# A decoder layer on one core: the feed-forward products of two heads by seven block products

## The chip, the cores and the metric

The kernel runs on one core of a Trainium2 chip. The core has five engines, each with its own instruction queue: TensorE (PE, matrix products; the loading of its stationary operand is shown apart as PEld), VectorE (DVE), ScalarE (ACT), GpSimd (POOL) and SyncE (SP, which here only issues transfers). They wait for one another by semaphores. TensorE writes to PSUM[...]; the other data lies in SBUF.

The metric is the device time of one execution, in microseconds. The kernel before took 1421.27 us (median of 3 runs, 1421.15 to 1422.03).

## The reference

The layer has 16 sequences of 256 tokens with 512 features. Cut to what matters:

```python
x = layernorm(x + attn(x))           # projections, short convolution, scan
y = causal_conv(v[i] * ctx[j], k) + skip * v[i] * ctx[j]
out[j] = sum_i y[i, j] * ctx[i]      # 8 x 8 pairs in each of 32 heads
x = layernorm(x + out)
base   = x @ W.T + b
logits = x @ gate_w.T + gate_b       # 8 experts
gates  = softmax(top_2(logits))
x = layernorm(base + sum_e gates[e] * (x @ A[e].T) @ B[e].T)
```

All of it is float32. The last three lines are the feed-forward part. For one head its main product is 128 tokens by 512 features by 512 outputs.

## The kernel before

The first part (up to about 750 us) works on groups of 512 tokens: projections, convolution, scan, output product. It already multiplies large matrices by seven block products in place of eight (lines 328 to 374), and the change does not touch it.

The second part is the loop at line 1232 over h = 0 to 31. A head here is 8 feature rows times 16 sequences, that is 128 tokens. Each iteration works on two heads at once: on the cross products of head h, and on the feed-forward part of head f = h - 1. An iteration has two halves, for two halves q of the batch. The instructions of an engine run in the order in which the loop writes them; the kernel sets that order itself, and no scheduler moves them.

One iteration, engine by engine:

* TensorE turns v of head h + 1 (`turned_v`, L147), multiplies the last two row blocks of the feed-forward product of the head before (`feed_forward`, L1227), turns its gates (`turned_gates`, L1217), begins the convolution with a shared product, the seed (L1012), adds the low-rank part (`lora`, L1223), and convolves: four full 128 x 128 products (L1030) and twelve quadrants of 64 x 64 (L1045). Then the second half: logits and low-rank inputs of head f into the tile gl (L1193), first row block (L1227), seed, second row block, and again four full products and twelve quadrants.
* VectorE multiplies the finished convolution by the context and sums it (`multiplied` L1080, `reduced` L1090, for both halves), finishes the feed-forward result of an earlier head (`finish`, L1151), makes the products of the next head (L157, twice), and computes the gates (L1118 to L1138).
* ScalarE copies turned tiles to SBUF (L149, L1219), copies the seed to another bank in two halves (`spread_seed`, L1019), squares for the norms (L1181, L1108) and scales the result that is stored (`store`, L1161).
* GpSimd adds the residual (L1260), folds the squares (L1185), multiplies and adds the skip term (L949 to L967), prepares the next head's sums (xs L996, Td L1001, sk L932), and does the small steps of the norms (L1103 to L1111, L1156, L1212).

Two rules of order matter below. A seed goes to bank 3 of y, `spread_seed` copies it from there to bank 2, and the second full product of the convolution adds to bank 3, so it has to wait until the copies have read it. And y has one buffer of two tiles, y0 and y1 (four banks): a convolution can start only when VectorE's multiplications have read the one before.

[...] four banks for y, two for the pool `ps_t` (gl and the turned gates), one for the turned v (`vp`) and one for the feed-forward result (`base`), both in `ps_b`.

In the gates the eight logits lg of each token are compared with one another (two comparisons, L1127 and L1128, of 128 x 64 elements); both operands are the same tile in SBUF.

Of the kernel before, what the change touches and what calls it, by code (L numbers as in the profile page):

```python
# [14 lines left out]
P = 128  # L15
# [57 lines left out]
def decoder_kernel(  # L73
# [842 lines left out]
    with ExitStack() as s2:  # L916
# [90 lines left out]
        def seeded(y, T, xs, q, apart=False):  # L1007

            seed = bank_of(y, 3)
            if apart:  # L1010
                seed = ps_b.tile([P, BQ * NH * NH], F32, tag="base", name="yc")
            nc.tensor.matmul(seed, T[:, SHARED_AT, :], xs[:, q], start=True, stop=True)  # L1012
            return seed
# [6 lines left out]

        def convolve(y, kv, T, Td, q, between=None, late=False, early=None, ahead=None):

# [45 lines left out]
            if late:  # L1068
                for n, (lb, mb) in enumerate(FIRST if ahead is None else AHEAD):
                    if n == 0 and ahead is not None:  # L1070
                        ahead()
                    if n == 1 and early is not None:
                        early()
                    if n == 3 and between is not None:
                        between()
                    full(lb, mb, T[:, FULL_AT[lb, mb], :])
# [23 lines left out]
        def centred_squares(src, total, tag, between=None):  # L1100

            nm = p2.tile([P, 1], F32, tag=f"nm_{tag}", name=f"nm_{tag}")
            nc.gpsimd.tensor_scalar(nm, total, -1.0 / D, None, ALU.mult)  # L1103
            if between is not None:
                between()
            sq = p2.tile([P, D], F32, tag="sq", name="sq")
            var = p2.tile([P, 1], F32, tag=f"var_{tag}", name=f"var_{tag}")
            nc.scalar.activation(sq, src, AF.Square, bias=nm, accum_out=var)  # L1108
            rs = p2.tile([P, 1], F32, tag=f"rs_{tag}", name=f"rs_{tag}")
            nc.gpsimd.tensor_scalar(var, var, 1.0 / D, LN_EPS, ALU.mult, ALU.add)  # L1110
            nc.gpsimd.tensor_tensor(rs, var, nhalf[:, 0:1], ALU.pow)  # L1111
            return nm, rs

        def gates(gl, rs, room):


            lg = p2.tile([P, NE], F32, tag="lg", name="lg")
            nc.vector.scalar_tensor_tensor(lg, gl[:, 0:NE], rs, gb_bc, ALU.mult, ALU.add)  # L1118
            nm = p2.tile([P, 1], F32, tag="nm", name="nm")
# [4 lines left out]
            own = lg.unsqueeze(2).to_broadcast(sq)  # L1124
            other = lg.unsqueeze(1).to_broadcast(sq)
            cmp = room.rearrange("p (a two b) -> p a two b", two=2, b=NE)
            nc.vector.tensor_tensor(cmp[:, :, 1, :], other, own, ALU.is_equal)  # L1127
            nc.vector.tensor_tensor(cmp[:, :, 0, :], other, own, ALU.is_gt)  # L1128
            nc.vector.tensor_tensor(cmp[:, :, 1, :], cmp[:, :, 1, :], tri, ALU.mult)
            rank = p2.tile([P, NE], F32, tag="rank", name="rank")  # L1130
            nc.vector.tensor_reduce(rank, cmp, AX.XY, ALU.add)
# [15 lines left out]

        def finish(h, base, rs, between=None):
            x3 = p2.tile([P, D], F32, tag="x3", name="x3")
            total = p2.tile([P, 1], F32, tag="sum_c", name="sum_c")  # L1150
            nc.vector.scalar_tensor_tensor(  # L1151
                x3, base, rs, b_bc, ALU.mult, ALU.add, accum_out=total
            )
            nm, rs = centred_squares(x3, total, "c", between)
            nb = p2.tile([P, 1], F32, tag="nb", name="nb")
            nc.gpsimd.tensor_tensor(nb, nm, rs, ALU.mult)  # L1156
            return h, x3, nb, rs
# [15 lines left out]
        def ahead():  # L1173
            vT_ahead.append(turned_v(vns.pop(0), ps_b, "vp"))
            vns.append(load_v(2))
            cTs.append(load_c(2))
# [12 lines left out]
        def products_with_gates(o_l, sq):  # L1189

            gl = ps_t.tile([P, NG + 2 + 2 * NE * NE], F32, tag="tr", name="gl")
            for kc in range(KD):
# [12 lines left out]
        def spread_of(gl, m2):  # L1205
# [4 lines left out]
            )  # L1210
            rs = p2.tile([P, 1], F32, tag="rs_b", name="rs_b")
            nc.gpsimd.tensor_tensor(rs, var, nhalf[:, 0:1], ALU.pow)  # L1212
            return rs

        def turned_gates(xa, at=None):
            xat = (at or ps_t).tile([ER, P], F32, tag="vp" if at else "tr", name="xat")
            nc.tensor.transpose(xat, xa.rearrange("p e r -> p (e r)"), ident)  # L1217
            xaT = p2.tile([ER, P], F32, tag="xaT", name="xaT")
            nc.scalar.copy(xaT, xat)  # L1219
            return xaT  # L1220

        def lora(base, turned):
            nc.tensor.matmul(base, turned[0], w_lb, start=False, stop=True)  # L1223

        def feed_forward(base, o_l, kcs, first=False):
            for kc in kcs:
                nc.tensor.matmul(  # L1227
                    base, o_l[:, kc, :], w_f[:, kc, :], start=(first and kc == kcs[0]), stop=False
                )

        last, done, rest = None, None, None
        for h in range(HX):
            nxt, ff = h + 1 < HX, last is not None
            (kv, T), cT, vT = kvs.pop(0), cTs.pop(0), vT_next
# [6 lines left out]
            if h:  # L1241
                if nxt:
                    v_after = turned_v(vns.pop(0), ps_b, "vp")
                    kvs.append(load_T(h + 1))
                    if h + 2 < HX:
                        vns.append(load_v(h + 2))
                        cTs.append(load_c(h + 2))
                if rest is not None:
                    base, o_r, xa = rest
                    feed_forward(base, o_r, (2, 3))  # L1250
                    turned = turned_gates(xa)
                seed = seeded(y, T, xs, 0, h == 1)
                spread_seed(y, seed, h == 1)
                if rest is not None:
                    lora(base, [turned])
            if ff:
                for i, pr in zip(order, prs):
                    reduced(pr, red_f, 1, i)
                o_l = p2.tile([P, NL, P], F32, tag="ol", name="ol")
                nc.gpsimd.tensor_tensor(  # L1260
# [5 lines left out]
                sq, folded = squares(o_l)  # L1266
            if done is not None:
                ready = finish(*done, folded)
            else:
                ready = None  # L1270
                if ff:
                    folded()
            red = p2.tile([P, NQ, NL, BQ * NH], F32, tag="red", name="red")
            convolve(y, kv, T, Td, 0, late=h == 0, ahead=None if h else ahead)
# [4 lines left out]
            if nxt:  # L1279
                kv_n, T_n = kvs[0]  # L1280
                cT_n, (vT_next, v_n, kept) = cTs[0], v_after
                if h:
                    behind = products(v_n, cT_n, kv_n, 0, kept=kept)
            skips = []

# [10 lines left out]
            y = new_y()  # L1296

            def meanwhile():
                skips.append(skip_term(cT, ws, behind))

            meanwhile()
            o = with_residual(skips[0], vT)
            if ff:
                gl, m2 = products_with_gates(o_l, sq)
                rs = spread_of(gl, m2)
                base = ps_b.tile([P, D], F32, tag="base", name="base")
                feed_forward(base, o_l, (0,), True)
            if nxt:
                seed = seeded(y, T, xs, 1, h == 0)
            if ff:  # L1310
                feed_forward(base, o_l, (1,) if nxt else (1, 2, 3))
            if ready is not None:
                store(*ready)
            if nxt:
                spread_seed(y, seed, h == 0)
# [7 lines left out]
            if ff:  # L1323
                xa = gates(gl, rs, gl[:, NG + 2 :])
            if nxt:
                convolve(y, kv, T, Td, 1)
                rest = (base, o_l, xa) if ff else None
            else:
                turned = []
                y.append(ps_t.tile([P, BQ * NH * NH], F32, tag="tr", name="y2"))  # L1330
                convolve(
                    y, kv, T, Td, 1, lambda: lora(base, turned), True,
                    lambda: turned.append(turned_gates(xa, ps_b)),
                )
            if ff:
                done = (h - 1, base, rs)
            last = (o, red, y, cT)
# [3 lines left out]
        tr = ps_t.tile([P, KD, P], F32, tag="tr", name="tr")  # L1341
        gl = ps_b.tile([P, NG + 2 * NE * NE], F32, tag="vp", name="gl")
        o_l = {}
# [48 lines left out]
        contracted(y_f[0], (0, 1))  # L1392
        ready = finish(*done)
        base = ps_b.tile([P, D], F32, tag="base", name="base")
        contracted(y_f[2].unsqueeze(1), (2,))
        contracted(y_f[1][:, 1:2, :], (3,))
        norms_and_gates(0, 1)
# [4 lines left out]
        _, rs = layer_norm_stats(nc, p2, nhalf, tr.rearrange("p c l -> p (c l)"), "b")  # L1402
        xaT = turned_gates(gates(gl, rs, gl[:, NG:]))
        store(*ready)
        nc.tensor.matmul(base, xaT, w_lb, start=False, stop=True, skip_group_check=True)
# [81 lines left out]
```

## Time and profile before

| | |
|---|---|
| Median of the runs | 1421.27 us |
| The profiled execution | 1421.88 us |
| Its span, first to last instruction | 1420.1 us |
| Granted TensorE clock | 0.998 |
| TensorE busy | 1405.9 us (99%), 6882 records |
| VectorE busy | 1191.5 us (84%) |
| GpSimd busy | 492.1 us (35%); 350.2 of the 600 us from 800 to 1400 |
| ScalarE busy | 415.0 us (29%) |
| One iteration of the loop (1014.37 to 1034.77) | 20.40 us |

How to read it: a float32 product shows as two records on TensorE. Its records overlap, since their ends are modelled, so the time that a product takes is read from one start to the next, not from its duration. "Idle before" is the time in which an engine had nothing to run, with the instruction that ended the wait. In timelines the columns are start, duration, engine, line, operation, output and inputs, shapes, count of merged instructions.

### The profile page before, as it was taken

How to read it: one execution, taken by the hardware profiler on the slowest of the kernel's cores; microseconds unless marked ns; L12 is line 12 of the kernel's file. 1: busy time of each engine (PE TensorE's matmuls, PEld its weight loads, DVE VectorE, ACT ScalarE, POOL GpSimd, SP SyncE). 2: the span in 40 equal slices, each digit the busy share in tenths (PEclk: the TensorE clock that was granted, in tenths of full speed). 3: DMA queues.
4: the chain of work that ended last, by engine and by line, in shares of the span. 5: the costliest groups of instructions: out<-in, count | busy, mean ns of one | idle time of the engine just before them, and what ended most of it. 6: DMA issues, size and time to landing. Idle time of an engine off the chain costs nothing.

```text
span 1420.1 us, 18821 instructions
## 1 busy us (share of the span) xinstructions
PE 1405.9 (99%) x6882; PEld 906.5 (64%) x6882; DVE 1191.5 (84%) x2133; ACT 415.0 (29%) x902; POOL 492.1 (35%) x662
## 2 busy tenths in 40 slices
PE   8999999999999999999999999999999999999997
PEld 7888888787888888888884444444444444444443
DVE  6988878888888787877858988898889889888986
ACT  2423323233232332332311323222322232222321
POOL 5450011110100201001004565556555655565562
PEclk9999999999999999999999999999999999999999
DMA  8013111120211201212003212221222122112200
GB/s 302 33 38 132 35 57 45 38 84 8 60 67 40 73 19 39 84 35 94 16 16 108 67 45 75 68 72 48 75 67 67 53 75 67 63 57 68 74 27 23
DMA packets 49164, 89.15 MB, mean 63 GB/s; under 512 B 8880, under 2 KB 13360, under 8 KB 49072
## 3 DMA queue, kind: packets, MB, share of 16 engines
q1 hardware_dynamic: 49072, 87.96, 19.6%
q8 instruction: 54, 0.88, 0.3%
q14 instruction: 38, 0.31, 0.1%
HBM read 70.62 MB, written 17.32 MB: 62 GB/s over the span
## 4 chain that ended last, share of the span: by engine, by line
PE 97%; DVE 1%; issue 1%; DMA 1%; SPq 0%; POOL 0%; POOLq 0%; ACT 0%; DVEq 0%
PE mm L330 21%; PE y L1030 15%; PE s L330 14%; PE y L1045 12%; PE base L1227 8%; PE s L782 6%; PE mm L782 6%; PE y L1012 4%; PE gl L1193 2%; PE base L1223 2%; PE tr L147 1%; PE xm L599 1%; PE mm L739 1%; PE mm L873 1%; PE s L873 1%
## 5 line engine op out<-in xcount | busy, mean ns | idle before, releaser
L1080 DVE TENSOR_TENSOR pr<-y,cT 128x1024 f32<-128x1024 f32 x126 | 148.1, 1217 | 57.8 <-PE y L1045 57.8
L1045 PE MATMUL y<-kv 64*64 64x512 f32 x1536 | 179.6, 598 | 0.0
L588 DVE SCALAR_TENSOR_TENSOR acc<-xi,wc,acc 128x512 f32<-128x512 f32 x192 | 142.6, 756 | 7.4 <-ACT acc L584 1.7
L1090 DVE TENSOR_REDUCE red<-pr 128x128 f32<-128x1024 f32 x126 | 147.1, 1208 | 0.0
L157 DVE TENSOR_TENSOR kv<-tr,cT 128x1024 f32<-128x1024 f32 x124 | 145.4, 1213 | 0.0
L1030 PE MATMUL y<-kv 128*128 128x512 f32 x272 | 128.0, 594 | 1.8 <-DVE pr L1080 1.7
L1045 PEld LDWEIGHTS y<-kv 64*64 64x64 f32 x1536 | 52.2, 132 | 119.0 <-issue 96.6
L1227 PE MATMUL base<-w_f,ol 128*128 128x512 f32 x248 | 124.0, 603 | 0.0
L1030 PE MATMUL y<-kv,Td 128*128 128x512 f32 x248 | 116.5, 592 | 0.0
L68 POOL TENSOR_TENSOR rs_a<-ve_a,nhalf 128x1 f32<-128x1 f32 x32 | 18.9, 592 | 242.1 <-DVE ve_a L66 242.1
L391 POOL TENSOR_TENSOR rstd<-ms,nhalf 128x4 f32<-128x4 f32 (+1 forms) x9 | 8.5, 948 | 251.7 <-DVE ms L389 251.7
L1260 POOL TENSOR_TENSOR ol<-o,red 128x512 f32<-128x512 f32 x31 | 39.3, 1269 | 160.2 <-DVE red L1090 160.2
L1030 PEld LDWEIGHTS y<-kv 128*128 128x128 f32 x272 | 50.9, 189 | 67.8 <-issue 34.1
L330 PE MATMUL mm<-XT,w_z 128*128 128x256 f32 x384 | 90.7, 379 | 0.0
L1030 PEld LDWEIGHTS y<-kv,Td 128*128 128x128 f32 x248 | 47.1, 190 | 59.3 <-issue 59.3
L1019 ACT COPY y<-y 64x512 f32<-64x512 f32 x120 | 67.0, 558 | 48.8 <-PE y L1012 46.9
L996 POOL TENSOR_TENSOR xs<-kv 128x512 f32<-128x512 f32 x63 | 80.2, 1272 | 0.1
L330 PEld LDWEIGHTS mm<-XT,w_z 128*128 128x128 f32 x384 | 73.0, 190 | 9.9
L330 PE MATMUL mm<-xnT,w_z 128*128 128x256 f32 x288 | 70.7, 382 | 0.0
L1227 PEld LDWEIGHTS base<-w_f,ol 128*128 128x128 f32 x248 | 42.4, 191 | 30.9 <-issue 30.9
L330 PE MATMUL s<-XT,w_xi 128*128 128x256 f32 x256 | 61.0, 380 | 0.4 <-DVE XT L226 0.2
L1012 PE MATMUL y<-xs,kv 128*128 128x512 f32 x120 | 61.3, 593 | 0.0
(283 smaller groups left out, 2786.8 us busy)
## 6 DMA issues: line engine op xcount, KB each, us to landing
cT<-in_ctxT SPq DMA_DIRECT2D x32, 384.0 KB
kv<-in_toep SPq DMA_DIRECT2D x32, 384.0 KB
xt<-in_x SPq DMA_DIRECT2D x32, 256.0 KB
spread<-both SPq DMA_DIRECT2D x32, 256.0 KB
first<-xt SPq DMA_DIRECT2D x32, 256.0 KB
vn<-first SPq DMA_DIRECT2D x32, 256.0 KB
out<-res SPq DMA_DIRECT2D x31, 256.0 KB
xnT<-in_xT SPq DMA_DIRECT2D x7, 1024.0 KB
```

Source lines behind the costliest of these rows:

```text
L157: last = nc.vector.tensor_tensor(kv[:, q, k * BQ : (k + NL // 2) * BQ], vT[:, q, blks].rearrange("p k (b i) -> p (k b) i", i=NH).unsqueeze ...
L330: nc.tensor.matmul(ps, w[:, p, a, kc, :], Xs[b][:, kc, :], start=start and kc == 0, stop=stop and kc == 1, skip_group_check=upon,)
L588: ins = nc.vector.scalar_tensor_tensor(acc, xi[:, :, k : k + S], wc[:, c, k : k + 1], acc, ALU.mult, ALU.add)
L782: nc.tensor.matmul(ps, own[a][c][:, n * P : (n + 1) * P], w_o[b][c], start=start and c == 0, stop=stop and c == HC - 1, skip_group_check=upon,
L996: return nc.gpsimd.tensor_tensor(xs[:, q], moving(kv, q, 0), moving(kv, q, 1), ALU.add)
L1012: nc.tensor.matmul(seed, T[:, SHARED_AT, :], xs[:, q], start=True, stop=True)
L1019: nc.scalar.copy(bank_of(y, 2)[b : b + HP], seed[a : a + HP])
L1030: nc.tensor.matmul(bank_of(y, lb), w, moving(kv, q, mb), start=not late and lb not in begun, stop=False, skip_group_check=True,)
L1045: return nc.tensor.matmul(bank_of(y, lb)[cols], T[rows, DIAGONAL_AT, (b - a) * HP : (b - a + 1) * HP], moving(kv, q, lb)[rows], start=star ...
L1080: nc.vector.tensor_tensor(pr.rearrange("p (k b j) i -> p k b j i", k=2, j=NH), y[i].rearrange("p k (b j i) -> p k b j i", j=NH, i=NH), cT[ ...
L1090: nc.vector.tensor_reduce(red[:, q, 2 * i : 2 * i + 2, :].rearrange("p k t -> p (k t)"), pr, AX.X, ALU.add)
L1227: nc.tensor.matmul(base, o_l[:, kc, :], w_f[:, kc, :], start=(first and kc == kcs[0]), stop=False)
```

## The change

Heads f = 1 to 30 are taken in pairs (1 and 2, 3 and 4, and so on); heads 0 and 31 stay as they were. The tokens of a pair form a matrix of two rows of blocks (head by half of the features), the weight one of two by two blocks (half of the features by half of the outputs). Their product is made by seven block products in place of eight. A block product is 128 tokens by 256 features by 256 outputs: two matmuls of 256 columns.

* Four differences of weight blocks, Tw, are made once by GpSimd (`weight_differences`, iterations 0 and 1).
* Four sums of token blocks, S1 to S4, are made by GpSimd for each pair (`sums`).
* The products accumulate in two banks, al and be. Three sums of 256 columns on VectorE (`common`) give the parts u and m that several of the four result blocks share. ScalarE first copies the first product to u.
* Three of the four result blocks need u or m. GpSimd scales it by the norm's factor of the head and adds the bias (`scaled`, a tensor_scalar and an addition), and `finish` takes the result in place of the bias.
* `finish` works on two halves of 256 columns in place of one of 512. The finish of a pair's first head stands at the end of the iteration behind the second convolution, and that of the second head where it was, in the next iteration.
* The low-rank product lora is split into four products of 256 columns for a pair.
* The gates write the logits twice: to a strip of the gl bank in PSUM (`seen`) and to lg in SBUF. The comparisons read one operand from each. The rank also goes to PSUM. The turned gates use the last 128 columns of the gl bank, and the turned v moves to the pool `ps_t`.

For a pair f, f + 1 the work is spread over three iterations. In iteration f + 2 the second head arrives: S1 and S3, then the first product, S2, the third and the fifth, S4. In iteration f + 3: the sixth product and the second, the common sums, the fourth, the low-rank part of the first head, the scalings, and finish of the first head. In iteration f + 4, in which the next pair's second head arrives: the seventh product, the low-rank part of the second head, its finish. Iteration 31 holds the rest of the last pair, in its last convolution.

The diff, cut to its core:

```diff
         def gates(gl, rs, room):
+            seen, rank = [room[:, 2 * NE * NE + n * NE :][:, 0:NE] for n in range(2)]
             lg = p2.tile([P, NE], F32, tag="lg", name="lg")
-            nc.vector.scalar_tensor_tensor(lg, gl[:, 0:NE], rs, gb_bc, ALU.mult, ALU.add)
+            for to in (seen, lg):
+                nc.vector.scalar_tensor_tensor(to, gl[:, 0:NE], rs, gb_bc, ALU.mult, ALU.add)
...
-            other = lg.unsqueeze(1).to_broadcast(sq)
+            other = seen.unsqueeze(1).to_broadcast(sq)
...
-        def finish(h, base, rs, between=None):
+        def finish(h, parts, rs, between=None):
             x3 = p2.tile([P, D], F32, tag="x3", name="x3")
-            nc.vector.scalar_tensor_tensor(
-                x3, base, rs, b_bc, ALU.mult, ALU.add, accum_out=total
-            )
+            for n, (cols, ps, own) in enumerate(parts):
+                nc.vector.scalar_tensor_tensor(
+                    x3[:, cols], ps, rs, own, ALU.mult, ALU.add, accum_out=total[:, n : n + 1]
+                )
             nm, rs = centred_squares(x3, total, "c", between)
...
+        def half_product(ps, a, w, start=False):
+            for kc in range(2):
+                nc.tensor.matmul(
+                    ps, a[:, kc, :], w[:, kc, :], start=(start and kc == 0), stop=(kc == 1),
+                    skip_group_check=True,
+                )
...
+            def common(self):
+                u, m = self.u, p2.tile([P, HD], F32, tag="m", name="m", bufs=1)
+                nc.vector.tensor_tensor(u, u, self.al[:, HI], ALU.add)
+                nc.vector.tensor_tensor(m, u, self.be[:, HI], ALU.add)
+                nc.vector.tensor_tensor(m, m, self.be[:, LO], ALU.add)
+                self.m = m
+
+            def scaled(self, what, head, cols, name):
+                to = p2.tile([P, HD], F32, tag=name, name=name, bufs=1)
+                nc.gpsimd.tensor_scalar(to, what, self.rs[head], None, ALU.mult)
+                nc.gpsimd.tensor_tensor(to, to, b_bc[:, cols], ALU.add)
+                return to
+
+            def scaled_first(self):
+                self.own = {1: self.scaled(self.u, 0, HI, "ua")}
+
+            def scaled_others(self):
+                self.own[2] = self.scaled(self.u, 1, LO, "ub")
+                self.own[3] = self.scaled(self.m, 1, HI, "mb")
...
         for h in range(HX):
...
-                    v_after = turned_v(vns.pop(0), ps_b, "vp")
+                    v_after = turned_v(vns.pop(0), ps_t, "tr")
...
-                if rest is not None:
-                    base, o_r, xa = rest
-                    feed_forward(base, o_r, (2, 3))
-                    turned = turned_gates(xa)
+                if opened is not None:
+                    opened.sixth()
+                if closing is not None:
+                    closing.seventh()
+                xaT = turned_gates(*turning) if turning is not None else None
...
                 seed = seeded(y, T, xs, 0, h == 1)
                 spread_seed(y, seed, h == 1)
+                if ready is not None:
+                    store(*ready)
...
+                if opened is not None:
+                    opened.second()
+                if closing is not None:
+                    closing.lora_of_second()
...
+                elif closing is not None:
+                    ready = closing.finish(1, folded)
+                    closing = None
...
+                if pair is not None and len(pair.o) == 2:
+                    pair.common()
+                    closing, pair = pair, None
...
                 gl, m2 = products_with_gates(o_l, sq)
+                if second:
+                    pair.first()
+                if closing is not None:
+                    closing.fourth()
+                    closing.scaled_first()
                 rs = spread_of(gl, m2)
...
             if ff:
-                xa = gates(gl, rs, gl[:, NG + 2 :])
+                if second:
+                    pair.sums_third()
+                if closing is not None:
+                    closing.scaled_others()
+                turning = gates(gl, rs, gl[:, NG + 2 :]), gl[:, XAT]
             if nxt:
                 convolve(y, kv, T, Td, 1)
+                if closing is not None:
+                    ready = closing.finish(0)
```

## The prediction

> **What bounds the kernel now.** I read the page first: busy shares, then the chain that ended last. Columns of the first four lines: engine, busy us (share), instructions.
>
> ```profile
> PE   1405.9 (99%) x6882; PEld 906.5 (64%) x6882; DVE 1191.5 (84%) x2133; ACT 415.0 (29%) x902; POOL 492.1 (35%) x662
> PE 97%; DVE 1%; issue 1%; DMA 1%; SPq 0%; POOL 0%; POOLq 0%; ACT 0%; DVEq 0%
> ```
>
> TensorE is the chain. The feed-forward part of it, L1227 and L1223, is 10%. Then I read the timeline of one head, engine by engine (start, duration, instruction):
>
> ```profile
> 1024.67 1.21 PE L1193 MATMUL gl<-w_gl,ol 128*128 128x137 f32 x8
> ...
> 1034.77 0.66 PE L147 MATMUL tr<-ident,vn 128*128 128x128 f32 x4
> 1035.27 1.88 PE L1227 MATMUL base<-w_f,ol 128*128 128x512 f32 x4
> 1036.98 0.27 PE L1217 MATMUL xat<-ident,xa 128*128 128x128 f32 x1
> 1037.09 1.02 PE L1012 MATMUL y<-xs,kv 128*128 128x512 f32 x2
> 1037.95 1.02 PE L1223 MATMUL base<-w_lb,xaT 128*128 128x512 f32 x2
> 1038.81 1.88 PE L1030 MATMUL y<-kv 128*128 128x512 f32 x4
> ```
>
> ```profile
> 1029.59 0.55 POOL L1212 TENSOR_TENSOR rs_b<-var_b,nhalf 128x1 f32<-128x1 f32 x1 [2.10 <-DVE var_b L1208]
> 1030.11 1.27 POOL L996 TENSOR_TENSOR xs<-kv 128x512 f32<-128x512 f32 x1
> 1031.34 0.72 POOL L1001 TENSOR_TENSOR Td<-kv 128x256 f32<-128x256 f32 x1
> 1032.03 1.49 POOL L932 TENSOR_TENSOR sk<-kv,skip_bc 128x512 f32<-128x512 f32 x1
> 1033.48 1.26 POOL L996 TENSOR_TENSOR xs<-kv 128x512 f32<-128x512 f32 x1
> ```
>
> ```profile
> 1035.52 0.59 ACT L149 COPY vT<-tr 128x512 f32<-128x512 f32 x1 [2.14 <-PE tr L147]
> 1037.29 0.27 ACT L1219 COPY xaT<-xat 128x128 f32<-128x128 f32 x1 [1.19 <-PE xat L1217]
> 1038.15 1.15 ACT L1019 COPY y<-y 64x512 f32<-64x512 f32 x2 [0.60 <-PE y L1012]
> ```
>
> ```profile
> 1031.95 0.22 DVE L1127 TENSOR_TENSOR gl<-lg 128x64 f32<-128x64 f32 x1
> 1032.21 1.40 DVE L1128 TENSOR_TENSOR gl<-lg 128x64 f32<-128x64 f32 x1
> ```
>
> See four things. A head is 20.40 us of TensorE without a gap. T below is the end of its second convolution, 1034.77 here. POOL's long run ends at 1034.74, exactly at T. The two L1019 copies end at 1039.30, and the full product behind them (second product of the last PE line) starts at 1039.67: only 0.37 to spare. And L1128 lasts 1.40 against 0.22 for the like L1127; it ends with POOL's L932. In head 31, where POOL is idle, L1128 took 0.23.
>
> [...]
>
> **The change part by part.** Call A the iteration in which a pair's second head arrives, B the next one (the pair's products end there).
>
> *TensorE.* A 512-column product starts 0.86 after the one before (1037.09 to 1037.95). A 256-column one is priced by L330: 12 records, two a product, from 301.66 to 304.25, so 0.432. Per pair, 10 x 0.858 = 8.58 becomes (14 + 4) x 0.432 = 7.78: 0.80 saved, 12 us over 15 pairs. By iteration: A holds ten small products (4.32 for 4.29, +0.03), B holds eight (3.46, -0.83). 14 B: -11.6; 13 A: +0.4. The ends differ. Iteration 2 has no products of a pair (-1.7), iteration 3 starts them (first half -1.7, second +0.9). Behind iteration 2's gap VectorE is late: from the quadrants' end it needs 9.4, TensorE 8.3. So I let -1.5 through of -2.5. Iteration 31: its last convolution carries five more small-pair steps for one 512 product, 10 x 0.432 - 0.86 = +3.5, on the tail's path; its first half saves 0.86. Together +2.6. Sum without new waits: -11.6 + 0.4 - 1.5 + 2.6 = -10.1.
>
> *VectorE.* Gates lose 1.17 (L1128 from 1.39 to 0.22) and 0.29 (L1133 from 0.46 to 0.17, as in head 31), and gain 0.22 for the second logits. The three common sums are as L360 to L362: 309.04 to 310.34, 1.3. A finish of two halves, each as L373's 0.33 plus a read of 0.07, is 0.80 for 0.66. B: from the first convolution's end 0.10 + 4.53 (multiply, reduce) + 0.06 + 2.27 + 2.41 (gates) + 0.80 = 10.17, against TensorE's 10.10. So VectorE is just on time; L1080's idle 1.79 pays for the common sums earlier in the head. The seventh product's wait for finish(0) (same bank) is then covered by the transposes' 0.49. From T to the seed TensorE's fill shrinks from 2.32 to 1.46; the first multiply has read y1 by T + 0.1 + 1.13, so the seed still doesn't wait. [...]
>
> *POOL.* Four sums of 0.73 (L1001's shape), weight differences of 5 us in iterations 0 and 1, and the first scaling fall in idle stretches of 2 to 5 us. Two scalings (scaled_others) do not: in B they stand behind the second xs, and finish(0)'s mean nm_c stands behind them. Each scaling is one tensor_scalar of 256 columns and an add of 0.73. The tensor_scalar: at least 0.19 (L1110, one column), at most 0.73 (two-input). [...] the 128x128 select at the start took 0.29, which scales to 0.40. I take 0.48.
>
> *The new queueing.* ScalarE's order after B is: Square of finish(0), vT, xaT, two L1019 copies. Before, that Square came later, behind a head's own. From T: POOL free at -0.03; two scalings 2 x (0.48 + 0.05 + 0.73) = 2.52, so 2.49; nm_c 0.24, 2.73; Square and its read 0.04 + 0.82, 3.59; vT 0.52; xaT 0.22; copies 1.15, ending at 5.48; then 0.2 to the full product, 5.68. TensorE gets there at 0.49 + 0.86 (seventh) + 0.11 + 0.86 (seed) + 0.86 (lora) + 0.86 (full) = 4.04. Stall 1.64 in each A behind a B, iterations 5, 7, ... 31: 14 x 1.6 = +22.4. What is behind the waiting Square needs nothing of it. Its bank is the one that the copies read, so it can't be begun earlier. Late next: nothing, since the products behind vT start at about 6, and POOL's next o_l addition at 4.8 finds the norm's steps just done. In the second halves A's new copy u (0.37, as L359) and the store's 0.75 stand in front of the copies and end 0.4 after the seed, but 1.72 of products cover it; B has neither. No wait. The buffers: turned v moves to the pool of gl, where the two then alternate, v freed by its second products before T as now, and the turned gates go into gl's own bank: no new wait. Loads and stores only shift on SP; two stores fall in A, none in B, 12 us ahead of the next loads.
>
> Sum: 22.4 - 10.1 = +12.3. The profiled span is 1420.1 in a run of 1421.88, the median 1421.27; the 1.8 outside is unchanged, so 1421.3 + 12.3, about 1433.
>
> **Rivals.** *Hidden chain, ends on the other side*: if the Square doesn't hold the copies (POOL done by T + 1.5), TensorE's saving is the result: 1421.3 - 10.1 = 1411. For it: TensorE is 97% of the chain. Against: POOL's run ending at T. It decides at a stall of 10.1/14 = 0.72, so a tensor_scalar of 0.02; even 0.19 gives 1.06 and 1426. Only an error of 0.9 in my chain turns the sign. *VectorE bounds*: [...] the seventh waits 1.0. With the Square's chain running until 5.68 anyway it adds nothing; without it 14 x 1.0 - 10.1 gives 1425. For it: VectorE's margin of -0.07. Against: head 31's 0.23. *POOL slower still*: a tensor_scalar of 0.73 gives a stall of 2.14 and 1441; one with a new cost above the two-input form, of 1.0, gives 1448.
>
> **How the numbers follow.** Chain as priced, tensor_scalar 0.19 to 0.73: 0.70 (1426 to 1441). Hidden chain: 0.17 (about 1407 to 1416). VectorE alone: 0.05. POOL slower: 0.08. The range 1413 to 1443 leaves about 0.11 below and 0.08 above. The likeliest case's own range is 1426 to 1441. A difference of 0.2% (2.8 us) is about what this kernel's runs can tell from none. Faster takes the hidden chain and a little of the rest, 0.19; same 0.03; slower 0.78.
>
> **What would show it.** Right: in every second head, the L1030 product after the seed waits about 1.6 for ScalarE's copies, with nm_c of finish(0) 2.7 after T on POOL; heads alternate between about 19.6 and 22.0 us; L1133 of after (is_gt) at 0.22. Wrong: heads of 19.6 and 20.4 (hidden), or the seventh product waiting for VectorE (second rival). [...] the order if ScalarE runs the Square after the copies.

## The result

| | before | after |
|---|---|---|
| Median of the runs | 1421.47 us | 1473.68 us (1470.21 to 1474.64) |
| Profiled execution, its span | 1421.88, 1420.1 us | 1470.21, 1468.4 us |
| Granted TensorE clock | 0.998 | 0.985 |

The ratio is 1.0362, with an interval of 1.0344 to 1.0381: slower by 52 us. The prediction was 1433, with a range that ended at 1443. The sign was right and the size was not.

### The profile page after: what moved, and what is told of

It reads as the page before. It is cut to its first block, busy times and chain, and to the rows that moved or that the text cites. A ratio compares the mean times of both kernels' runs of the same rounds, so it can differ in the third digit from the quotient of the medians.

```text
span 1468.4 us, 19593 instructions
## 1 busy us (share of the span) xinstructions
PE 1419.9 (97%) x7122; PEld 958.7 (65%) x7122; DVE 1177.0 (80%) x2270; ACT 419.9 (29%) x917; POOL 612.2 (42%) x816
## 4 chain that ended last, share of the span: by engine, by line
PE 71%; POOL 13%; DVE 10%; ACT 3%; issue 2%; DMA 0%; SPq 0%; POOLq 0%; DVEq 0%
PE mm L330 20%; PE s L330 13%; PE y L1030 9%; PE y L1045 6%; PE s L782 6%; PE mm L782 6%; DVE pr L1078 3%; POOL xs L996 3%; DVE red L1088 2%; DVE kv L157 2%; PE be L1260 2%; POOL sk L932 1%; POOL o L967 1%; PE gl L1198 1%; ACT y L1019 1%
## 5 line engine op out<-in xcount | busy, mean ns | idle before, releaser
L1030 PE MATMUL y<-kv 128*128 128x512 f32 x272 | 137.4, 619 | 32.0 <-ACT y L1019 30.0
L1030 PE MATMUL y<-kv,Td 128*128 128x512 f32 x248 | 130.4, 653 | 0.0
L1030 PEld LDWEIGHTS y<-kv,Td 128*128 128x128 f32 x248 | 52.3, 211 | 68.3 <-issue 63.9
L1019 ACT COPY y<-y 64x512 f32<-64x512 f32 x120 | 67.0, 558 | 38.8 <-PE y L1012 36.2
L1012 PE MATMUL y<-xs,kv 128*128 128x512 f32 x120 | 62.7, 604 | 0.8 <-POOL xs L996 0.7
L223 POOL TENSOR_TENSOR XT<-xnT 128x512 f32<-128x512 f32 x7 | 9.1, 1297 | 129.0 <-PE mm L782 129.0
L330 PEld LDWEIGHTS mm<-xnT,w_z 128*128 128x128 f32 x288 | 54.1, 190 | 10.0 <-issue 3.0
```

The lines of the kernel that those rows point to most:

```text
L330: nc.tensor.matmul(ps, w[:, p, a, kc, :], Xs[b][:, kc, :], start=start and kc == 0, stop=stop and kc == 1, skip_group_check=upon,)
L1019: nc.scalar.copy(bank_of(y, 2)[b : b + HP], seed[a : a + HP])
L1030: nc.tensor.matmul(bank_of(y, lb), w, moving(kv, q, mb), start=not late and lb not in begun, stop=False, skip_group_check=True,)
```

## The profile after

The page of the changed kernel, in the same two lines as before (busy shares; the chain that ended last):

```profile
PE 1419.9 (97%) x7122; PEld 958.7 (65%) x7122; DVE 1177.0 (80%) x2270; ACT 419.9 (29%) x917; POOL 612.2 (42%) x816
...
PE 71%; POOL 13%; DVE 10%; ACT 3%; issue 2%; DMA 0%; SPq 0%; POOLq 0%; DVEq 0%
```

GpSimd, which had no share of the chain, now has 13% of it. TensorE's busy time went up by 14 us, although the change removes products: something lengthens them. The costliest groups show where TensorE waits (after the second bar: its idle time, and what ended most of it):

```profile
L1030 PE MATMUL y<-kv 128*128 128x512 f32 x272 | 137.4, 619 | 32.0 <-ACT y L1019 30.0
```

These 30.0 us are 14 waits for the copies of the seed, one in each iteration in which a pair's second head arrives (A) behind one that closes a pair (B). One of them, on TensorE (start, duration, instruction, idle time ahead of it with its releaser); the second convolution of the head before ends at T = 1068.12:

```profile
1068.12 0.66 PE L147 MATMUL tr<-ident,vn 128*128 128x128 f32 x4
1068.62 1.03 PE L1260 MATMUL be<-Tw,ol 128*128 128x256 f32 x4
1069.48 0.27 PE L1222 MATMUL gl<-ident,xa 128*128 128x128 f32 x1
1069.59 1.07 PE L1012 MATMUL y<-xs,kv 128*128 128x512 f32 x2
...
1071.36 1.02 PE L1030 MATMUL y<-kv 128*128 128x512 f32 x2
1074.55 1.13 PE L1030 MATMUL y<-kv 128*128 128x512 f32 x2 [2.17 <-ACT y L1019]
1075.51 3.51 PE L1030 MATMUL y<-kv,Td 128*128 128x512 f32 x4
```

The same moment on GpSimd:

```profile
1066.76 1.27 POOL L996 TENSOR_TENSOR xs<-kv 128x512 f32<-128x512 f32 x1
1068.01 0.93 POOL L1317 TENSOR_SCALAR ub<-u,rs_h 128x256 f32<-128x256 f32 x1
1069.02 0.73 POOL L1318 TENSOR_TENSOR ub<-ub,b_bc 128x256 f32<-128x256 f32 x1
1069.72 0.92 POOL L1317 TENSOR_SCALAR mb<-m,rs_h 128x256 f32<-128x256 f32 x1
1070.73 0.72 POOL L1318 TENSOR_TENSOR mb<-mb,b_bc 128x256 f32<-128x256 f32 x1
1071.43 0.26 POOL L1102 TENSOR_SCALAR nm_c<-sum_c 128x1 f32<-128x1 f32 x1
```

And on ScalarE:

```profile
1071.73 0.72 ACT L1111 ACTIVATE sq<-x,nm_c 128x512 f32<-128x512 f32 x1 [5.00 <-POOL nm_c L1102]
1072.36 0.19 ACT L1111 ACTIVATION_READ_ACCUMULATOR sq<-x,nm_c 128x1 f32 x1
1072.57 0.59 ACT L149 COPY vT<-tr 128x512 f32<-128x512 f32 x1
1073.06 0.27 ACT L1224 COPY xaT<-gl 128x128 f32<-128x128 f32 x1
1073.35 1.15 ACT L1019 COPY y<-y 64x512 f32<-64x512 f32 x2
```

Read the three together, from the bottom up. TensorE's second full product waits for the L1019 copies. These stand on ScalarE behind the Square of the first head's finish, the Square waits for nm_c, and nm_c stands on GpSimd behind the two scalings. The queue that the prediction described is there, step for step. But L1317, priced at 0.48 us, takes 0.93, so nm_c ends at T + 3.57 in place of T + 2.73, and the product starts at T + 6.43 in place of T + 5.68.

The last line of TensorE shows something that the prediction did not have at all: the four records of two products take 3.51 us, which took 1.88 before. The busy time by stretches, with the granted clock (the third number from the end: 1.00 or about a half), says why:

```profile
1072.20:1074.55 2.35, 0.18 (x1) 0.00 (x0) 2.35 (x7) 2.27 (x7) 1.75 (x4) 1.00 0.38 133
1074.55:1075.51 0.96, 0.96 (x2) 0.49 (x3) 0.96 (x2) 0.96 (x2) 0.67 (x2) 1.00 0.00 0
1075.51:1078.96 3.45, 3.45 (x6) 0.91 (x4) 1.00 (x1) 0.96 (x3) 2.79 (x7) 0.52 0.20 76
1078.96:1081.70 2.74, 2.74 (x25) 0.79 (x24) 0.00 (x0) 0.19 (x1) 2.58 (x5) 0.99 0.04 9
```

About one microsecond behind this gap of 2.17 us, TensorE's clock falls to half, for 3.41 us, and comes back. The trace's record of the clock has eleven such stretches in the loop, each of 3.413 us and at 0.50; two of the thirteen A iterations ahead of the last head have none.

**The ledger**, from seed to seed (the starts of L1012), in spans. From a closing iteration's second seed (B) to the next first seed it is 9.45 us where it was 10.30: -0.85, so 13 times -11.1, and -0.5 ahead of head 31. A's first half is 12.61 us without a fall of the clock (+2.50) and 14.3 with one (+4.19), where it was 10.11: 2 x 2.50 + 11 x 4.19 = +51. Iterations 2 and 3 give -1.8. The first seed of all comes 0.7 us earlier (761.83 in place of 762.49), which is chance: in the runs below, with the same work ahead of it, it lies anywhere from 761.47 to 762.79. From head 31's first seed to the end it is 46.95 us (1421.47 to 1468.42) where it was 36.45: +10.5. With +0.9 spread over the rest the sum is +48.3, the difference of the spans.

The last head has its own new waits. On TensorE, and on GpSimd:

```profile
1433.63 1.89 PE L1260 MATMUL be<-Tw,S 128*128 128x256 f32 x8
1437.71 1.13 PE L1260 MATMUL al<-Tw,S 128*128 128x256 f32 x4 [2.19 <-POOL S L1278]
```

```profile
1436.42 0.55 POOL L1217 TENSOR_TENSOR rs_h<-var_b,nhalf 128x1 f32<-128x1 f32 x1 [1.55 <-DVE var_b L1213]
1436.93 0.72 POOL L1278 TENSOR_TENSOR S<-S,ol 128x256 f32<-128x256 f32 x1
```

The sixth product needs S2, and S2 stands in GpSimd's queue behind rs_h, which waits for VectorE. Nearer the end there are two more. The second line is of the kernel before:

```profile
1457.22 0.23 DVE L1123 SCALAR_TENSOR_TENSOR y<-y,rs_b,gb_bc 128x8 f32<-128x8 f32 x1 [2.01 <-PE y L1565]
1409.42 0.23 DVE L1118 SCALAR_TENSOR_TENSOR lg<-gl,rs_b,gb_bc 128x8 f32<-128x8 f32 x1 [0.67 <-POOL rs_b L68]
```

```profile
1453.74 0.33 PE L1557 MATMUL tr<-ident,ol 128*128 128x128 f32 x1 [0.74 <-DVE ol L1548]
```

The last head's logits waited 0.67 us for the norm's factor; now they wait 2.01 for a product of base. And TensorE waits 0.74 for ol (the last head's input of the feed-forward part), which VectorE makes behind the finishes of the last pair.

## The experiments

All of them start from the changed kernel unless their text says otherwise. Three theories were to be told apart. *Queue*: the stall comes from the order on GpSimd and ScalarE. *Clock*: the rest of the loop's loss is a fall of the clock that the stall brings about. *Work*: the seven products, or VectorE, cost the time themselves.

**The mean ahead of the scalings.** GpSimd's work stays the same; only nm_c of the first head is issued ahead of the two late scalings.

```diff
-                if closing is not None:
-                    closing.scaled_others()
...
-                    ready = closing.finish(0)
+                    ready = closing.finish(0, closing.scaled_others)
```

> The only edit: GpSimd makes the mean of the first head's finish before the two late scalings, not behind them. Theory (queue and clock): the Square no longer holds ScalarE's copies, so each of the 13 first halves of A loses its 2.5 us of wait and the 1.7 us of slow products, the last head 1.8; from the profiled 1470.2 us that is 52.7 less, 1417 to 1418. Rival (the added VectorE work, or where the finish stands on VectorE): the finish stays where it is, so the time stays above 1450. Rival (the pair's products as such, say bank waits): no change.

Measured: 1419.72 us, ratio 0.9988 (0.9981 to 0.9994). One A iteration, all engines in order of time (T = 1050.10):

```profile
1050.41 0.26 POOL L1102 TENSOR_SCALAR nm_c<-sum_c 128x1 f32<-128x1 f32 x1 [0.40 <-DVE x L1156]
1050.65 0.93 POOL L1317 TENSOR_SCALAR ub<-u,rs_h 128x256 f32<-128x256 f32 x1
...
1052.69 1.15 ACT L1019 COPY y<-y 64x512 f32<-64x512 f32 x2 [0.38 <-PE y L1012]
1053.35 1.88 PE L1030 MATMUL y<-kv 128*128 128x512 f32 x4
```

The copies now wait for the seed, as before the change, and the product does not wait. A's first half is 10.17 us. Putting one instruction ahead of four gives back 54 us, more than the whole loss, so the stall and what follows from it are the loop's loss. At head 31's first seed this kernel is 11.4 us ahead of the kernel before (1372.24 against 1383.62); the last head then loses 8.9.

**The Square behind the copies.** GpSimd keeps the late order; on ScalarE the Square of the first head's finish is issued where its store stands, behind the copies.

```diff
-                    ready = closing.finish(0)
+                    ready = finish_first(closing.f, closing.parts(0), closing.rs[0])
...
-                    store(*ready)
+                    store(*ready())      # Square, norm and store, behind spread_seed
```

> The changed kernel, but the Square of the first head's finish is issued on ScalarE behind the copies of the seed; GpSimd's order and VectorE's stay. Theory (ScalarE's strict order carries GpSimd's lateness to TensorE): as in the first run, 1417 to 1420, although the scalings still stand ahead of the mean. Rival (GpSimd's lateness acts by another way, the next residual or the next sums): above 1440.

Measured: 1420.63 us, ratio 0.9994 (0.9985 to 1.0003), and A's first half again 10.17. One A iteration (T = 1049.25):

```profile
1051.83 1.15 ACT L1019 COPY y<-y 64x512 f32<-64x512 f32 x2 [0.64 <-PE y L1012]
...
1052.55 0.27 POOL L1102 TENSOR_SCALAR nm_c<-sum_c 128x1 f32<-128x1 f32 x1
...
1052.90 0.72 ACT L1111 ACTIVATE sq<-x,nm_c 128x512 f32<-128x512 f32 x1
```

nm_c ends as late as in the changed kernel (T + 3.57), and in the loop it costs nothing. The scalings do harm only by ScalarE's order: in the changed kernel the copies stood behind a Square that waited 5.00 us for nm_c, and here they start 0.72 us ahead of nm_c (1051.83 and 1052.55).

The profiled execution lost time at another place, its last head:

```profile
1386.19 2.07 PE L1267 MATMUL al<-Tw,S 128*128 128x256 f32 x4 [2.72 <-POOL S L1285]
1388.20 4.91 PE L1045 MATMUL y<-kv 64*64 64x512 f32 x24
```

Behind the wait for S2, here 2.72 us, the clock was at half for 6.83 us, and these products took 2.07 and 4.91 us (1.13 and 2.81 in the first experiment's kernel). Its last head is 48.27 us long, there it is 45.36.

**Work in the gap.** If the clock falls because TensorE idles, more work there must make the kernel faster. Two products of 512 columns are added in each A iteration ahead of the waiting one, into a bank that is overwritten later; nothing needs their result.

```diff
+                for _ in range(fill):            # 2 in iterations 5, 7, ..., else 0
+                    nc.tensor.matmul(
+                        bank_of(y, 0), ident, moving(kv, q, 0), start=True, stop=True,
```

> The changed kernel with two products of 512 columns more in each A behind a B, between the first full product and the one that waits for ScalarE (they go to a bank that is overwritten afterwards). ScalarE's chain is as before, only TensorE is busy in 1.7 of the 2.3 us. Theory (TensorE's clock falls because TensorE was idle): the wait stays, the slow products go: 11 slow stretches x 1.7 less than the profiled 1470.2, about 1451, faster by added work. Rival (the products are slow because of what runs beside them, transfers or GpSimd): 1470 to 1475. Rival (TensorE, not ScalarE, sets the pace there): 22 us more, 1495.

Measured: 1452.7 us, ratio 1.0222 (1.0207 to 1.0238). TensorE in an A iteration:

```profile
1065.84 1.88 PE L1057 MATMUL y<-kv,ident 128*128 128x512 f32 x4
1068.19 1.13 PE L1030 MATMUL y<-kv 128*128 128x512 f32 x2 [0.47 <-ACT y L1019]
1069.15 1.88 PE L1030 MATMUL y<-kv,Td 128*128 128x512 f32 x4
```

The product starts no earlier (A's first half is 12.61, the number without a fall), but the two products behind it take 1.88 in place of 3.51, and no stretch of the loop is at half clock (the granted clock of the run is 0.997, where it was 0.985). 28 useless products made the kernel 21 us faster. That is the clock's share of the loss: about 19 us by the ledger of the profiled execution (11 x 1.69), and 21 by the medians.

**The scaling with two inputs.** The tensor_scalar is replaced by a tensor_tensor of the same result, with the factor spread over the columns.

```diff
-                nc.gpsimd.tensor_scalar(to, what, self.rs[head], None, ALU.mult)
+                nc.gpsimd.tensor_tensor(to, what, self.rs[head].to_broadcast([P, HD]), ALU.mult)
```

> The changed kernel with the scaling as a two-input multiplication by the norm's factor spread over the columns (0.73 us of GpSimd by the row of Td) in place of the one-input one (0.93). Theory: two scalings stand in the chain, so the wait of each A shrinks by 0.4 to 0.5 from 2.3, 13 x 0.45 = 6 us; the idle time may then be short enough for the clock to stay up in some of the 11 stretches: 1445 to 1466. If the spread operand costs more, slower than 1474.

Measured: 1442.71 us, ratio 1.015 (1.0135 to 1.0165). One A iteration:

```profile
890.01 0.61 POOL L1317 TENSOR_TENSOR ub<-u,rs_h 128x256 f32<-128x256 f32 x1
...
895.90 1.13 PE L1030 MATMUL y<-kv 128*128 128x512 f32 x2 [1.46 <-ACT y L1019]
896.87 1.88 PE L1030 MATMUL y<-kv,Td 128*128 128x512 f32 x4
```

0.61 us in place of 0.93, and the wait shrinks by 0.71, twice the difference and a little more. The waits of the thirteen A iterations are 1.46 to 1.50 us here, and behind none of them does the clock fall (granted clock 0.997), so 2 x 0.3 us on GpSimd are worth 31 us to the kernel. The time came out a little below the expected bracket.

**One scaling ahead, one behind.** A dose between the changed kernel and the first experiment: ub ahead of nm_c, mb behind it.

```diff
-                    ready = closing.finish(0)
+                    ready = closing.finish(0, closing.scaled_last)    # mb's scaling alone
```

> Only one of the two late scalings (u's) stays ahead of the mean on GpSimd; that of m goes behind it. Theory (GpSimd's queue sets the copies, and the clock falls only behind a long gap): one scaling is 0.93 + 0.08 + 0.73, about 1.7 us, so the wait of the full product falls from 2.2 to about 0.5 and the first half behind a closing iteration from 12.6 us without a fall of the clock to about 10.9, without falls. From the version with both behind the mean, 1419.7 + 13 x 0.73 = about 1429. Rival (the clock falls behind any gap in this place): 11 more x 1.7, about 1448. Rival (the wait is all or nothing, set by something else than the length of the queue): 1420 or 1470.

Measured: 1428.42 us, ratio 1.0052 (1.0036 to 1.0067). TensorE in an A iteration:

```profile
1057.29 1.13 PE L1030 MATMUL y<-kv 128*128 128x512 f32 x2 [0.47 <-ACT y L1019]
1058.25 1.88 PE L1030 MATMUL y<-kv,Td 128*128 128x512 f32 x4
```

The wait is 0.47, as expected, A's first half 10.89 (1054.03 to 1064.92), and the clock stays up (1.88 us for the two products behind the wait, granted clock 0.997). Over the doses of 0, 1 and 2 scalings ahead, the first half without a fall is 10.17, 10.89 and 12.61: the first scaling costs 0.72 since part of it is hidden, the second its whole 1.72.

**The logits in SBUF only.** The first experiment's kernel, with the comparisons reading lg twice. It tests the prediction's second rival, in which the seventh product waits for VectorE, and what the second logits are worth.

```diff
-            for to in (seen, lg):
-                nc.vector.scalar_tensor_tensor(to, gl[:, 0:NE], rs, gb_bc, ALU.mult, ALU.add)
+            nc.vector.scalar_tensor_tensor(lg, gl[:, 0:NE], rs, gb_bc, ALU.mult, ALU.add)
...
-            other = seen.unsqueeze(1).to_broadcast(sq)
+            other = lg.unsqueeze(1).to_broadcast(sq)
```

> The version with the mean ahead of both scalings (1419.7), with the comparisons reading lg in SBUF twice and no second logits. Theory [...]: the second comparison takes 1.4 us again, the gates are 1.2 longer, the finish of the first head ends about 1.35 after the end of the second convolution, and the seventh product waits for it about 0.9 in each of 14 iterations: about 1432. Rival (VectorE's order has the room anyway): 1420.

Measured: 1432.10 us, ratio 1.0075 (1.0062 to 1.0089). On VectorE and TensorE:

```profile
1051.76 1.39 DVE L1132 TENSOR_TENSOR gl<-lg 128x64 f32<-128x64 f32 x1
...
1055.48 1.13 PE L1259 MATMUL be<-Tw,ol 128*128 128x256 f32 x4 [0.49 <-DVE x L1155]
```

The comparison is slow again (1.39 us with both operands in SBUF; with one in PSUM, L1133 of the changed kernel took 0.23 in every head), and the seventh product waits for finish. From B's second seed to A's first it is 10.31 us (1046.35 to 1056.66) in place of 9.45. The second logits are worth 12 us to the pairs: without them the whole gain of seven products is gone. Why the comparison takes longer with both operands in SBUF was not shown.

**The logits in PSUM, alone.** The same part in the kernel before, with heads one by one and eight block products.

```diff
-            nc.vector.scalar_tensor_tensor(lg, gl[:, 0:NE], rs, gb_bc, ALU.mult, ALU.add)
+            for to in (seen, lg):
+                nc.vector.scalar_tensor_tensor(to, gl[:, 0:NE], rs, gb_bc, ALU.mult, ALU.add)
```

> The kernel before with one part of the change alone: the second logits in PSUM, read by the comparisons; heads one by one with eight block products as before. The two comparisons take 0.23 and 0.17 in place of 1.40 and 0.46, so VectorE has about 1.2 us more room in every head, and its wait ahead of the multiplications grows by that. TensorE had no wait for VectorE before, so the time stays, 1421.3 within 1 us. Rival (VectorE's lateness cost something in the loop already): 1421.3 less up to 30 x 0.1, 1418.

Measured: 1422.07 us, ratio 1.0005 (0.9997 to 1.0013): no difference. VectorE, in the head that the prediction showed:

```profile
1032.23 0.23 DVE L1130 TENSOR_TENSOR gl<-gl,lg 128x64 f32<-128x64 f32 x1
...
1034.63 2.35 DVE L1080 TENSOR_TENSOR pr<-y,cT 128x1024 f32<-128x1024 f32 x2 [0.69 <-PE y L1045]
```

The comparison takes 0.23 and VectorE is 1.2 us earlier, but it only waits for the convolution instead. The same edit is worth nothing here and 12 us there: it depends on whether the engine's slack has been spent.

**The last head: S2 early.** From the first experiment's kernel; in head 31 alone, S2 is made right behind S1 and S3.

```diff
                     pair.sums_first()
+                    if not nxt:
+                        pair.sums_second()
...
-                if second:
+                if second and nxt:
                     pair.sums_second()
```

> The version with the mean ahead of both scalings (1419.7); in the last head alone GpSimd makes S2 right behind S1 and S3, ahead of the skip terms. If the sixth product's wait of 2.26 us for S2 lies on the end's path, 2 us go, less some 0.3 that the later gates take back: about 1417.7. If VectorE sets the tail, 1419.7 stays.

Measured: 1417.67 us, ratio 0.9973 (0.9963 to 0.9983). The number is the expected one, but the trace does not carry the reason in full. TensorE in the last head:

```profile
1387.11 1.09 PE L1045 MATMUL y<-kv 64*64 64x512 f32 x8 [0.69 <-ACT one L1061]
1388.90 1.13 PE L1260 MATMUL al<-w_f,ol 128*128 128x256 f32 x4 [0.70 <-DVE u L1310]
```

The wait of 2.26 is gone, and two waits of 0.7 stand in its place. From the seed of head 31 to the turning of the last gates (L1222) it is 35.65 us, where the first experiment's kernel has 36.48: 0.8 of the 2.26 us, and no more, are seen to come from there. Another 0.6 lies ahead of the last head, where the two kernels do not differ. Behind the gates 0.4 is lost again, by the clock: it goes to half at 1407.65 here and at 1409.89 there, and the last low-rank product takes 2.07 in place of 1.63. So the profiled executions differ by 1.0 us and the medians by 2.05, and the rest of the medians' difference is in no trace.

**The last head: a tile of its own for base.** In the tail the logits gl and the result base are the two banks of one tile, and the logits (L1123) waited 2.01 us for the last product of base. Here base gets tile y1.

```diff
-        first_y = ps_y.tile([P, 2, D], F32, tag="y0", name="y0")
-        base, gl = [first_y[:, n, :] for n in range(2)]
+        gl = ps_y.tile([P, 2, D], F32, tag="y0", name="y0")[:, 1, :]
...
+        base = ps_y.tile([P, 2, D], F32, tag="y1", name="y1")[:, 0, :]
         norms_and_gates(0, 1)
-        feed(0)
         norms_and_gates(2, 3)
-        for k in (1, 2, 3):
+        for k in range(4):
             feed(k)
```

> As the version with S2 made early, and in the tail the feed-forward result base gets a tile of its own (y1) in place of the second bank of the logits' tile; its first product moves behind the logits' products. The logits then wait for the norm's factor and no longer for the products of base: 1.3 us less, about 1416.4. If the wait is not the tile's, about 1417.7.

Measured: 1415.76 us, ratio 0.9961 (0.9949 to 0.9974), the fastest of all. On VectorE and TensorE:

```profile
1402.96 0.23 DVE L1123 SCALAR_TENSOR_TENSOR y<-y,rs_b,gb_bc 128x8 f32<-128x8 f32 x1 [0.67 <-POOL rs_b L68]
...
1405.58 0.33 PE L1222 MATMUL y<-ident,xa 128*128 128x128 f32 x1 [0.53 <-DVE xa L1142]
...
1406.27 1.13 PE L1585 MATMUL y<-w_lb,xaT 128*128 128x512 f32 x2 [0.35 <-ACT xaT L1224]
```

The logits wait 0.67, for the norm's factor, as in the kernel before. There is a gain that was not expected, too: with a gap of 0.53 us ahead of it in place of 2.74, the last low-rank product takes 1.13, where it took 2.07 in the kernel with S2 early. The record of the clock has the reason: there the clock is at half from 1407.65 on, ahead of that product (1407.93), and here from 1408.50 on, behind it.

**The finishes behind the gates.** From the kernel just told of: the two finishes of the last pair, 1.9 us of VectorE between the last multiplications, are moved behind the last head's gates.

```diff
-        ready = [pair.finish(0)]
-        ready.append(pair.finish(1))
-        for one in ready:
+        for one in [pair.finish(head) for head in range(2)]:
             store(*one)
```

> As the version with S2 early and base in a tile of its own (1415.8), with the two finishes of the last pair moved behind the last head's gates. They stand on VectorE between the last multiplications, 4 x 0.48 = 1.9 us; the last multiplication starts when TensorE has ended, 0.85 earlier than now. If this is what is left of the last head's loss, 1414.9; if the two results' norms and stores are then late and set the end, 1416 or more.

Measured: 1418.46 us, ratio 0.9979 (0.9971 to 0.9988): slower than without the move. VectorE, near the end:

```profile
1410.22 0.75 DVE L1585 SCALAR_TENSOR_TENSOR x<-y,rs_b,b_bc 128x512 f32<-128x512 f32 x1 [3.41 <-ACT res L1166]
```

The last multiplication did move ahead, but the last head's x then waits 3.41 us for the buffer that the store of the pair's first head (L1166) still reads. The second case of the expectation held, by a way that it did not name: not the stores themselves but the reuse of their buffer is late.

## Why the prediction was wrong in size

Step by step, by its own sum (spans: +12.3 forecast, +48.3 measured).

* **TensorE's saving: right.** B's part was forecast at -0.83 and is -0.85; iterations 2 and 3 gave -1.8 for a forecast of -1.5.
* **VectorE's part: right.** The comparisons, the common sums and the finish took what the prediction gave them: VectorE left finish(0) for its next instruction at T + 0.13 (forecast T + 0.07), and the seventh product did not wait. The experiment with the logits in SBUF only shows that this hung on the second logits: with a comparison of 1.39 us in place of 0.23 the pair loses 0.86, which the rival put at 1.0.
* **The new queueing: mechanism right, its size wrong.** The term that failed is the tensor_scalar: taken at 0.48, an estimate, bounded by 0.19 and 0.73, measured at 0.93. The upper bound was the error. The prediction held that one input can't cost more than two, and no row of before shows this operation at size. As measured, a tensor_scalar with a factor for each partition takes longer than either two-input form (0.61 with a spread factor, 0.73 with two full inputs). Why it does stays open. With it the delay is 2.33 us rather than 1.64, and A's first half grows by 2.50: +0.8 in each of 13, about 11 us of the miss.
* **A term that was missing: the clock.** The sum priced an idle gap at its own length. Behind 11 of the 13 gaps of 2.16 to 2.19 us TensorE ran 3.413 us at half clock, which took 1.69 us more each: 18.6 us. "Late next: nothing" looked for instructions that come late behind the stall, and not for a TensorE that runs slower. The rival "POOL slower still", 1448 at a tensor_scalar of 1.0, lacked this term, too.
* **The last head: three waits were missing.** Forecast, from head 31's first seed on, +3.5 for the five extra steps and +1.6 for the stall; measured +10.5. By stretches of TensorE (L1012, L1198, L1557, the end; before L1012, L1193, L1379, the end): from the seed to the logits +2.05, the stall. From there to the tail +5.94, of which 2.19 are the wait for S2 (the experiment won back only some 0.8 of it, since VectorE is then late); that leaves 3.75 for the five steps, close to the forecast. In the tail +2.52, where the sum had nothing: 1.3 for the shared tile of base and gl (2.01 where before waited 0.67), 0.7 for ol behind the finishes, and some tenths of small ones, among them a last product at half clock (1.33 in place of 1.13).

These terms, 11 + 19 + 5, make up all but 1 of the 36 us between the forecast and the measured spans. The median lies 3.5 us above the profiled execution, which is the fastest of its kernel. The granted clock of that one was 0.985, and of the other three 0.984, 0.982 and 0.982, with spans 2.5, 4.4 and 4.5 us longer. At 1.69 us and 3.413 us of half clock for a fall, two more would lengthen a run by 3.4 us and lower its clock by 0.002, so a different number of falls would explain most of the spread; that is an estimate from these figures, since only one execution has a trace.

The *hidden chain* rival would have missed, too: with the stall taken away, the kernel took 1419.7 and not 1411, because of the last head.

## What to carry to other kernels

Before work is put on a lightly used engine, find the small instruction behind it that another engine's queue waits for, and issue that first: here one mean, put ahead of two scalings, was worth 54 us. Price an idle gap of a bound TensorE with its clock as well: against 10.17 us without a gap, A's first half was 1.7 us longer with a gap of 1.46 us, and 4.1 longer with one of 2.17 and the fall behind it. An operation that the trace doesn't show has no upper bound from its neighbours (a tensor_scalar taken as at most 0.73 us took 0.93); where a forecast hangs on it, the range has to reach further.

## What the runs showed of the hardware

* **When the clock falls.** In the changed kernel TensorE's gaps in the thirteen A iterations ahead of the last head are 2.16 to 2.19 us long. Behind eleven of them the clock was at half for 3.413 us, and behind two, those that ended at 855.14 and 1162.88, it was not. The falls began from 0.1 us ahead of the gap's end (fall at 1205.32, product at 1205.40) to 1.3 us behind it (fall at 1119.98, product at 1118.71). The gaps of 1.70 and 2.19 us in head 31 brought none, nor did that of 2.26 in the last head of the first experiment, nor the shorter ones of two other runs: 1.46 to 1.50 with the scaling of two inputs, 0.44 to 0.47 with work in the gap. With the Square behind the copies, 2.72 us in the last head were followed by 6.83 us at half clock. So of gaps between 2.1 and 2.3 us some brought a fall and some did not; what decides between them was not shown. Both kernels end at half clock, from 1414.4 on before and from 1461.3 on after.
* **What the falls cost the loop.** Two heads would take 42.5 us without a fall (9.45 + 12.61 + 10.31 + 10.15); with one they take 44.2. From the start of one fall to the next it is 44.37 us, and once 85.33, where a gap ahead brought none (1162.88).
* **GpSimd at 128 x 256, float32**: tensor_scalar with a factor for each partition 0.93 us (changed kernel, L1317), tensor_tensor with that factor spread over the columns 0.61 (the scaling with two inputs, L1317), tensor_tensor with two full inputs 0.73 (changed kernel, L1318).
